# The half-swap of a rotated projection, issued on GpSimd's queue in place of the sync queue

## The chip, the cores and the metric

The kernel runs on one core of one Trainium2 chip. The metric is the device time of one execution in microseconds; the time of a kernel is the median of its runs. A core has five engines that run their own instruction streams: TensorE (PE in the profile; its weight loads are shown apart as PEld), VectorE (DVE), ScalarE (ACT), GpSimd (POOL) and SyncE (SP, which here only issues transfers). They wait for each other through semaphores. A transfer (DMA) is an instruction in the stream of the engine that issues it; the moving itself is done by 16 DMA engines, which all queues share.

## The reference

Four blocks follow each other, each with a layer norm ahead of it and added to the stream x (1024 rows of 512):

```python
x = x + attn_a(layernorm(x))      # 32 heads of 16, 8 key/value groups
x = x + ffn(layernorm(x))         # dense layer + the two best of 8 low-rank experts
x = x + attn_b(layernorm(x))      # the second attention, below
x = x + ffn(layernorm(x))
```

The change is in `attn_b`. Its weights are small whole numbers with a scale for each 128 rows of a column, its 32 query heads of 128 share 8 key/value heads, and queries and keys are rotated before the scores:

```python
w = (qw.astype(float32) - 8.0) * repeat(scales, 128, axis=0)   # _dequant_matmul
q, k, v = x @ w_q, x @ w_k, x @ w_v
def rotate_half(x):
    x1, x2 = split(x, 2, axis=-1)
    return concatenate([-x2, x1], axis=-1)
q = q * cos + rotate_half(q) * sin                             # and k the same
scores = q @ k.T / sqrt(128)                                   # causal
out = dequant_matmul(softmax(scores) @ v, qw_o, scales_o)
```

The second half of a head's 128 numbers thus has to come to where the first half stands, and the other way round.

## The kernel before

The program is one launch. The first attention and the first feed-forward block take the first 480 us or so; then the second attention begins to overlap with the end of the feed-forward block, and its heads fill the stretch from about 535 to 1350 us; the last feed-forward block follows.

**Layout.** In the second attention a projection is kept transposed: the 128 numbers of a head lie on the 128 partitions, the 1024 tokens along the free dimension, worked on in two halves of 512. Swapping the halves of the head dimension therefore means moving partitions 64 to 127 to partitions 0 to 63 and back, for 512 tokens of 4 bytes each: two transfers of 128 KB for each half of the tokens.

**One projection.** `whole_numbers` (700) loads a weight tile `r` of whole numbers on GpSimd's queue (L705) and GpSimd turns it into the number minus 8, tile `w` (L706). `r` has one buffer for each kind, `w` two. `scaled` (803) forms 512 tokens of the projection: for each of four slices of the contraction, two matmuls (the stream is held as a high and a low part; `exact`, L798 and L799) go into a PSUM bank `pp`, and the bank is multiplied by its scale into the tile `acc`, the first by ScalarE (L810), the next three by VectorE, which add (L812). `rotated` (815) does this for the two token halves: it takes an `acc` tile, forms it, swaps its halves into a tile `turned` by the two transfers L822 and L823, and then multiplies `acc` by the cosine into the result (L824), `turned` by the sine (L825) and adds (L826). These three run on GpSimd, except for query head 0, where VectorE does them. The sign of the rotation is in the sine table. `keys` (829) and `queries` (833) call `rotated`, the one for a group's key head, the other for a query head; `values` (838) uses `scaled` alone and then a ScalarE copy. There are 8 key heads and 32 query heads, two halves each: 80 pairs of transfers, 160 in all. `acc` and `turned` come from the pool `b_work`, which has two buffers of each; a buffer of `acc` is free again when the two transfers and L824 have read it, and `values` uses the same two.

**One head.** For each block t of 128 query rows, in the order 0, 6, 1, 7, 2, 4, 3, 5: scores against all keys up to the block (`probabilities` 861: matmuls L869, VectorE mask and maximum L877, ScalarE exponential L881), division (`divided` 884: L885, L886), and `placed` (890): VectorE transposes the probabilities in 32x32 blocks (L900), and for each pair of row blocks SP issues four transfers that bring the 32-row strips together (L911). `context` (936) multiplies them with the values (L949, bank `pc`) and writes the result as a high and a low part (L961, L962); `project_out` (967) multiplies with the output weights (L798 and L799 again, bank `py`) and adds to the output: VectorE L983 for three of four slices, ScalarE L987 and GpSimd L988 for the last.

**What sets the order.** TensorE's order is written out by hand: the head loop (1098) works through the row blocks and fills in between, by a cost account, from two lists: `short` (projections of coming heads and the output projections) and `long` (context products). The projection of query head n + 1 is inserted ahead of the others in head n; a key group's projection is added at the first head of a group for the next group, its values at the third. Each item is a generator; what stands in it behind a `yield` runs when it is advanced the next time, and the swap of a half stands behind the last `yield` of `scaled`. So where a query's projection is put ahead of a key's that has one half finished, this half's swap comes after the query's, and its `acc` buffer is held until then. The order on the other engines is set by the scheduler, which knows what each instruction depends on. Each engine and each queue works strictly in its own order: an instruction that waits holds up all that stand behind it.

**Queues.** On SP's queue in this stretch stand the swaps L822 and L823, the placing transfers L911 and a few others; on GpSimd's the weight loads L705, beside its own instructions L706, L824 to L826 and L988.

Of the kernel before, what the change touches and what calls it, by code (L numbers as in the profile page):

```python
# [41 lines left out]
def kernel(  # L42
# [28 lines left out]
    nc = tc.nc  # L71
# [601 lines left out]
    def attention_b():  # L673
# [5 lines left out]
        with ExitStack() as ph:  # L679
# [123 lines left out]
            def scaled(acc, w, scale, half):  # L803

                tok = ts(half, C)
                for c in range(NC_):
                    pp = ac_ps.tile([P, C], F32, tag="acc", name="pp")
                    exact(pp, w[:, c], x_hl[:, 0, c, tok], x_hl[:, 1, c, tok])
                    if c == 0:
                        nc.scalar.activation(acc, pp, AF.Copy, scale=scale(c))  # L810
                    else:
                        nc.vector.scalar_tensor_tensor(acc, pp, scale(c), acc, ALU.mult, ALU.add)  # L812
                    yield 2 * FAST

            def rotated(dst, w, scale, engines=(nc.gpsimd, nc.gpsimd)):

                for half, eng in enumerate(engines):
                    tok = ts(half, C)
                    acc = work.tile([P, C], F32, tag="acc", name="acc")
                    yield from scaled(acc, w, scale, half)  # L820
                    turned = work.tile([P, C], F32, tag="turned", name="turned")
                    nc.sync.dma_start(turned[0:64], acc[64:128])  # L822
                    nc.sync.dma_start(turned[64:128], acc[0:64])  # L823
                    eng.tensor_tensor(dst[:, tok], acc, cos_sb[:, tok], ALU.mult)  # L824
                    eng.tensor_tensor(turned, turned, sin_sb[:, tok], ALU.mult)  # L825
                    eng.tensor_tensor(dst[:, tok], dst[:, tok], turned, ALU.add)  # L826
                    yield 0

            def keys(g):
                kTs[g] = work.tile([P, S], F32, tag="kT", name=f"kT_{g}")  # L830
                yield from rotated(kTs[g], wks.pop(g), lambda c: k_sc[:, c, g : g + 1])

            def queries(n):
                qTs[n] = work.tile([P, S], F32, tag="qT", name=f"qT_{n}")
                engines = 2 * (nc.gpsimd if n else nc.vector,)
                yield from rotated(qTs[n], wqs.pop(n), lambda c: q_sc[:, c, n : n + 1], engines)
# [448 lines left out]
```

## Time and profile before

| what | value |
|---|---|
| median of 3 runs | 1445.62 us (1443.53 to 1448.45) |
| the profiled execution: time, span | 1443.47 us, 1441.6 us |
| busy over the span: PE, DVE, ACT, POOL | 1387.7, 1188.9, 868.2, 596.9 us |
| second attention, 535 to 1350 us: PE, DVE, ACT, POOL busy of 815 us | 793.62, 724.45, 541.86, 530.07 us |
| swap transfers (160), median from issue to landing | 3.1 us |
| mean granted TensorE clock | 0.994 of full speed |

Times in the profile are us from the start of the span. "L822" is line 822 of the kernel. "SPq" and "POOLq" are the queues on which SP and GpSimd issue transfers; the duration shown for a transfer in a timeline is the time for which its issue holds the issuing stream, not that of the moving. `turned<-acc` reads: writes tile `turned`, reads tile `acc`. In brackets behind an instruction stands the time that its engine was idle ahead of it, and what ended that. Weight loads of TensorE overlap its matmuls. GpSimd's busy time doesn't count its issues of transfers.

### The profile page before, as it was taken

How to read it: one execution, taken by the hardware profiler on the slowest of the kernel's cores; microseconds unless marked ns; L12 is line 12 of the kernel's file. 1: busy time of each engine (PE TensorE's matmuls, PEld its weight loads, DVE VectorE, ACT ScalarE, POOL GpSimd, SP SyncE). 2: the span in 40 equal slices, each digit the busy share in tenths (PEclk: the TensorE clock that was granted, in tenths of full speed). 3: DMA queues.
4: the chain of work that ended last, by engine and by line, in shares of the span. 5: the costliest groups of instructions: out<-in, count | busy, mean ns of one | idle time of the engine just before them, and what ended most of it. 6: DMA issues, size and time to landing. Idle time of an engine off the chain costs nothing. (4 is left out here: it accounts for less than half of the span.)

```text
span 1441.6 us, 21145 instructions
## 1 busy us (share of the span) xinstructions
PE 1387.7 (96%) x6711; PEld 882.1 (61%) x6711; DVE 1188.9 (82%) x2491; ACT 868.2 (60%) x1642; POOL 596.9 (41%) x505
## 2 busy tenths in 40 slices
PE   6999999999999998899999999999999999999888
PEld 4444444444444545677677777777777777777664
DVE  4799979979893658789898998999998998989774
ACT  2166757757677325676576676676666676666630
POOL 4200000000000616566666767657667566645230
PEclk9999999999999998999999999999999999999999
DMA  4352423324240213655566565655655655565711
GB/s 126 61 100 48 69 42 56 62 35 70 48 134 2 86 66 98 153 138 148 140 147 156 126 149 145 149 143 140 149 140 145 145 137 141 139 137 119 193 57 59
DMA packets 113183, 158.47 MB, mean 110 GB/s; under 512 B 35008, under 2 KB 86912, under 8 KB 112944
## 3 DMA queue, kind: packets, MB, share of 16 engines
q1 hardware_dynamic: 106252, 135.51, 40.3%
q0 software_dynamic: 6752, 21.57, 5.6%
q8 instruction: 54, 0.88, 0.2%
q14 instruction: 57, 0.47, 0.1%
q10 hardware_dynamic: 68, 0.03, 0.0%
HBM read 33.03 MB, written 6.05 MB: 27 GB/s over the span
## 5 line engine op out<-in xcount | busy, mean ns | idle before, releaser
L387 ACT ACTIVATE pT<-st 128x512 f32<-128x512 f32 x512 | 264.6, 603 | 128.7 <-PE st L383 109.6
L343 DVE TENSOR_REDUCE m<-sc 128x1 f32<-128x512 f32 x512 | 319.8, 682 | 25.8 <-PE st L375 19.8
L869 PE MATMUL sc<-kT,qT 128*128 128x512 f32 (+3 forms) x768 | 292.0, 489 | 2.4 <-POOL qT L826 1.3
L881 ACT ACTIVATE x_sb<-x_sb,m 128x768 f32<-128x768 f32 (+7 forms) x256 | 197.0, 769 | 120.4 <-DVE m L877 117.7
L949 PE MATMUL pc<-xT,v_sb 128*128 128x256 f32 (+1 forms) x1024 | 240.4, 361 | 14.2 <-DMA xT<-blocks 14.0
L886 ACT ACTIVATE x_sb<-x_sb,total 128x768 f32<-128x768 f32 (+7 forms) x256 | 195.5, 771 | 70.4 <-DVE total L885 69.0
L949 PEld LDWEIGHTS pc<-xT,v_sb 128*128 128x128 f32 x1024 | 190.7, 189 | 49.5 <-issue 17.2
L877 DVE CUSTOM_DVE_ANT_0 x_sb<-sc,causal 128x768 f32<-128x768 f32 (+7 forms) x256 | 191.4, 748 | 27.5 <-PE sc L869 26.1
L334 PE MATMUL sc<-ks,qs 64*128 64x512 f32 x512 | 186.7, 448 | 5.4 <-DVE m L343 2.6
L798 PE MATMUL pp<-x_hl,w 128*128 128x512 f32 x384 | 183.5, 478 | 2.2 <-ACT acc L810 1.6
L869 PEld LDWEIGHTS sc<-kT,qT 128*128 128x128 f32 x768 | 139.0, 192 | 74.5 <-issue 61.7
L383 PE MATMUL st<-ms_q,ones 64*128 64x512 f32 x512 | 178.0, 413 | 0.8 <-DMA ms_q<-mT 0.7
L375 PE MATMUL st<-qs,ks 64*128 64x512 f32 x512 | 176.0, 423 | 1.4
L334 PEld LDWEIGHTS sc<-ks,qs 64*128 64x128 f32 x512 | 83.9, 184 | 146.3 <-DVE m L343 129.6
L900 DVE STREAM_TRANSPOSE blocks<-x_sb 128x640 f32<-128x640 f32 (+3 forms) x128 | 133.2, 1041 | 27.1 <-ACT x_sb L886 21.2
L799 PE MATMUL pp<-x_hl,w 128*128 128x512 f32 x384 | 153.0, 399 | 2.2 <-DVE x_hl L756 2.2
L127 POOL DMA_DIRECT2D shared<-in_b_base_dram x1 | 0.5, 547 | 367.3 <-DVE m L343 367.3
L812 DVE SCALAR_TENSOR_TENSOR acc<-pp,q_sc,acc 128x512 f32<-128x512 f32 x192 | 140.7, 733 | 10.4 <-ACT acc L810 7.4
L706 POOL TENSOR_SCALAR w<-r 128x512 fp32r<-128x512 int32 x80 | 119.5, 1493 | 71.0 <-PE pp L799 47.0
L408 PE MATMUL po<-pT,v_sb 128*32 128x512 f32 x1024 | 136.6, 605 | 0.0
L824 POOL TENSOR_TENSOR qT<-acc,cos_sb 128x512 f32<-128x512 f32 x62 | 80.1, 1292 | 131.9 <-DVE acc L812 120.8
L798 PE MATMUL py<-ctx,w 128*128 128x512 f32 x256 | 133.0, 520 | 1.2 <-DVE xT L136 0.7
(178 smaller groups left out, 2196.8 us busy)
## 6 DMA issues: line engine op xcount, KB each, us to landing
xT<-blocks SPq DMA_DIRECT2D x128, 240.0 KB, 4.4
xT<-blocks SPq DMA_DIRECT2D x128, 176.0 KB, 3.4
turned<-acc SPq DMA_DIRECT2D x160, 128.0 KB, 3.1
pT<-x_sb SPq DMA_DIRECT2D x128, 112.0 KB, 3.6
qs<-q_hl SPq DMA_DIRECT2D x128, 64.0 KB, 2.4
qs<-shared SPq DMA_DIRECT2D x128, 64.0 KB, 2.6
r<-in_qwq_dram POOLq DMA_DIRECT2D x32, 256.0 KB, 3.6
r<-in_qwo_dram POOLq DMA_DIRECT2D x32, 256.0 KB, 3.6
```

Of the source, the lines that this page charges most:

```text
L334: nc.tensor.matmul(sc, qs[pair % NS][rows, jj, ts(t, P)], ks[pair // 2 % NS][rows, ts(half, C)], start=True, stop=True,)
L343: nc.vector.tensor_reduce(ms[pair][:, at : at + 1], sc, AX.X, ALU.max, negate=True)
L375: nc.tensor.matmul(st, ks[pair // 2 % NS][rows, ts(kt, P)], qs[pair % NS][rows, u // 2, ts(u % 2, C)], start=True, stop=False,)
L383: nc.tensor.matmul(st, ones[rows], ms_q[pair % 2][rows, u // 2, ts(u % 2, C)], start=False, stop=True)
L387: nc.scalar.activation(pTs[pair, kt][:, u], st, AF.Exp, scale=DA**-0.5)
L798: nc.tensor.matmul(ps, lhsT, high, start=True, stop=False)
L799: nc.tensor.matmul(ps, lhsT, low, start=False, stop=True)
L869: nc.tensor.matmul(sc[:, k0:k1], qT[:, ts(t, P)], kT[:, k0:k1], start=True, stop=True)
L877: nc.vector.tensor_tensor_reduce(p, sc[:, :keys], causal[:, S - keys :], -1.0, BIG, ALU.add, ALU.min, m)
L881: nc.scalar.activation(p, p, AF.Exp, bias=m, scale=-1.0, accum_out=total)
L886: nc.scalar.activation(p, p, AF.Copy, scale=total)
L949: nc.tensor.matmul(pc[:, 2 * P * i + lo : 2 * P * (i + 1)], v_sb[:, k, ts(g, DB)], some, start=(k == 0), stop=(k == 2 * pair + 1),)
```

## The change

The two transfers that swap the halves are issued by GpSimd and no longer by SP. Nothing else is edited.

```diff
@@ rotated @@
                     acc = work.tile([P, C], F32, tag="acc", name="acc")
                     yield from scaled(acc, w, scale, half)
                     turned = work.tile([P, C], F32, tag="turned", name="turned")
-                    nc.sync.dma_start(turned[0:64], acc[64:128])
-                    nc.sync.dma_start(turned[64:128], acc[0:64])
+                    nc.gpsimd.dma_start(turned[0:64], acc[64:128])
+                    nc.gpsimd.dma_start(turned[64:128], acc[0:64])
                     eng.tensor_tensor(dst[:, tok], acc, cos_sb[:, tok], ALU.mult)
                     eng.tensor_tensor(turned, turned, sin_sb[:, tok], ALU.mult)
                     eng.tensor_tensor(dst[:, tok], dst[:, tok], turned, ALU.add)
                     yield 0
```

In the scheduled program TensorE's order is the same as before. SP's order is that of before without the 160 swaps. On GpSimd each pair now stands among its other instructions, in most places right ahead of the L824 of the same half; some neighbours change places with each other by one to three, and on VectorE and ScalarE a few by up to four.

## The prediction

> **What bounds the kernel now.** I read the page first (engine shares, clock row, issues), then the table of windows over the second attention (535 to 1350 us), then the waits of that stretch, then the groups of the tile `turned`, and last the timeline at the places where TensorE stands still.
>
> ```profile
> PE 1387.7 (96%) x6711; PEld 882.1 (61%) x6711; DVE 1188.9 (82%) x2491; ACT 868.2 (60%) x1642; POOL 596.9 (41%) x505
> ...
> turned<-acc SPq DMA_DIRECT2D x160, 128.0 KB, 3.1
> ...
> r<-in_qwo_dram POOLq DMA_DIRECT2D x32, 256.0 KB, 3.6
> ```
>
> The windows, with each engine's busy us in each stretch, then granted clock, DMA share and GB/s:
>
> ```profile
> core 0: us, PE busy (x) PEld busy (x) DVE busy (x) ACT busy (x) POOL busy (x), PEclk, DMA share, GB/s
> 535.00:620.00 85.00, 74.84 (x280) 51.18 (x279) 68.56 (x144) 51.23 (x94) 52.30 (x42) 0.92 0.48 122
> ...
> 823.00:1026.00 203.00, 201.38 (x847) 150.73 (x846) 184.39 (x391) 137.23 (x256) 141.03 (x117) 1.00 0.59 145
> ...
> 1230.00:1350.00 120.00, 115.02 (x484) 85.88 (x482) 103.89 (x229) 80.42 (x151) 62.99 (x52) 1.00 0.57 134
> ```
>
> TensorE is the bound: 201.38 of 203 us in the steady state (heads run alike from about 620 to 1230 us), at full granted clock. The change moves no matmul, so it acts only through TensorE's idle time: 10 us in the first stretch, under 2 us per 203 us after it, 5 us at the end. GpSimd has 62 us free in 203.
>
> The waits of 535 to 1350 us that touch the swap or SP's queue (us in total, times, longest):
>
> ```profile
> POOL turned L825 <- DMA turned<-acc: 38.8, 26, 4.3
> ...
> PE pc L949 <- DMA xT<-blocks: 12.1, 12, 1.7
> ...
> ACT acc L810 <- DMA turned<-acc: 3.2, 5, 1.3
> ...
> PE sc L869 <- POOL qT L826: 1.3, 1, 1.3
> ```
>
> The reader sees two kinds. A late swap holds an `acc` buffer (two exist), so that L810, which starts the next projection half, waits. And the context product L949 waits for the 32x32 blocks that SP places (L911), behind the swaps on the same queue.
>
> **The change part by part.** *SP loses 160 issues, GpSimd gains them.*
>
> ```profile
> L822 SPq DMA_DIRECT2D turned<-acc x80: 461/510/662, 536.2 to 1335.7; - x80
> L823 SPq DMA_DIRECT2D turned<-acc x80: 586/596/1659, 536.7 to 1336.3; - x80
> ...
> DMA to landing us min/median/max: 2.2/3.1/4.1
> ```
>
> ```profile
> L705 POOL DMA_DIRECT2D r<-in_qwo_dram x32: 549/597/601, 489.4 to 1339.3; - x32
> ```
>
> SP is relieved of 80 x (0.510 + 0.596) = 88 us. On GpSimd no SBUF-to-SBUF transfer stands in the trace; a plain load holds its queue 0.549 to 0.601 us and a four-piece one 0.80. I take 0.55 (nearest: a plain two-dimensional transfer), bounds 0.46 (SP's shortest) and 0.80. So 1.1 us a pair and 88 us in all. Eight heads hold 20 pairs (16 query, 4 key halves): 141 + 22 = 163 of 203 us. Behind each pair L824 (1.29 us) runs, then L825 needs the landing: 0.55 + 3.1 - 1.1 - 1.29 = 1.26 us of standing still where nothing is ordered between, at most 25 us in 20 pairs: 188 of 203. GpSimd is then nearly full, but still under TensorE. What waits behind on it are L706 and L705 (weights of a coming head), L988 (the output's add) and the last of the rotation, L826. From L826 of a query's second half to the first score product of its head 4.4 to 7.8 us lie in the steady state, for a key some 45 us. I charge 1.1 to 3 us of delay against these: nothing, hidden by the running head's matmuls. Where GpSimd is already late by more than that cover, TensorE waits.
>
> *Steady state, six places.* In the third head of a group (heads 6, 10, 14, 18, 22, 26) the key's second half, finished by TensorE but not yet swapped, holds one `acc` buffer, and both query halves go through the other one. Head 14:
>
> ```profile
> 892.94 0.60 SPq L823 DMA_DIRECT2D turned<-acc  x1
> ...
> 895.76 0.69 ACT L810 ACTIVATE acc<-pp,q_sc 128x512 f32<-128x512 f32 x1
> ...
> 896.50 0.19 PEld L798 LDWEIGHTS py<-ctx,w 128*128 128x128 f32 x1 [0.81 <-ACT acc L810]
> ...
> 904.25 0.60 SPq L823 DMA_DIRECT2D turned<-acc  x1
> ...
> 911.89 1.10 PE L949 MATMUL pc<-xT,v_sb 128*128 128x256 f32 x4 [0.91 <-DMA xT<-blocks]
> ```
>
> L810 starts 2.82 us after the second swap's issue, as it lands (slack 0.0 to 0.5 us at the six). GpSimd came to this swap with 0.77 us to spare, behind the key's first half, whose own pair now puts 1.1 to 1.4 us more ahead: 0.65 late. The landing on its queue: 3.6 us (L705) against 2.7 for transfers of 256 KB on SP's says +0.9; that the swaps now pass the placing transfers on the other queue, at best from median 3.1 to 2.2, says -0.9. I take +0.6, since the placing group at 888.72 was already issued well before. Loss 1.25 us. Then SP's gain: two pairs stand on SP just before the placing at 904.95, whose transpose (L900) ended at 903.87; without them it starts up to 1.08 us sooner, and the wait at 911.89 (0.91; the six sum to 5.25) can go. I take 0.7. Net 6 x 0.55 = +3.3; bounds 6 x (0.35 - 0.9 - 0.87) = -8.5, taken as -5.25, since a wait cannot give back more than it is, and 6 x (0.65 + 0.9) = +9.3.
>
> The Trainium skill ("DMA: Bandwidth & Descriptors", Specifications) puts the first byte at some 1 us for GpSimd's path and 0.6 for SP's; an estimate by that page would be +0.4 in place of +0.6 here, 1.2 us less over the six. The trace has no GpSimd transfer of this kind to decide it.
>
> *Start, heads 0 and 1.* Here GpSimd also converts four weights, and heads wait on each other directly:
>
> ```profile
> 557.52 0.69 ACT L810 ACTIVATE acc<-pp,q_sc 128x512 f32<-128x512 f32 x1 [1.33 <-DMA turned<-acc]
> ```
>
> SP issued the key's swap at 552.85 and the query's at 555.23, each as its `acc` was ready. GpSimd in the new order ends L705 at 553.55, issues the key's pair (to 554.65), runs L824 and L706 (to 557.45) and only then the query's: 2.2 us late. So L810 at 557.52 is 0.7 late, the next one at 559.10 about 2.5, and the score product at 562.07, which already waits 0.82 us for the query's L826, 1.3. All three lie on TensorE's order: +4.5, bounds +2 (they overlap) and +7 (the granted clock here is 0.73 to 0.93 between 545 and 575 us, and longer gaps lower it further).
>
> *End, head 31.* The last query half is ready at 1332.4, but SP is in a placing group until 1335.56:
>
> ```profile
> 1335.67 0.55 SPq L822 DMA_DIRECT2D turned<-acc  x1
> ...
> 1344.10 1.77 PE L869 MATMUL sc<-kT,qT 128*128 128x512 f32 x4 [1.28 <-POOL qT L826]
> ```
>
> GpSimd is free (it runs L824 at 1332.46), so the swap is 3 us earlier and this wait goes: -1.28. Late next are the blocks (1.64 us at 1339.70), which don't depend on it.
>
> *Order.* TensorE's is the same; the scheduler moves some GpSimd, DVE and ACT instructions by one to four places (a transpose L900 four places earlier at each of the six heads). Nothing: TensorE's waits for these are 0.2 us and below apart from those above.
>
> **Sum.** +3.3 + 4.5 - 1.3 = +6.5. On the profiled execution (1443.47: span 1441.6 and 1.87 around it) that is 1449.97; it lies 2.15 under the median of three, 1445.62, so against the median 1452.1: I predict **1452**.
>
> **The rivals.** *SP's relief decides (faster).* Six waits of L949 (5.25) and head 31 (1.28) go, and the landings are as soon as SP's: 1445.6 - 6.5 = 1439. Place: L911 of the six heads. It decides if the swap at L810 lands no later than now, so that the 1.25 and the 4.5 fall away to near nothing. For it: SP holds two pairs right before the placing. Against: GpSimd works in order and came with 0.77 us to spare.
>
> *All hidden (same).* The early loss is at its least (+2), the six places come out even, the end gives 1.3: 1446.3. For it: 62 us free per 203; against: the zero slack of `acc`.
>
> *GpSimd falls behind (slower).* If issue costs 0.80 and every L825 stands 1.3 us, a pair costs 2.9: 141 + 58 = 199 of 203 us, and in the third head of a group, with three pairs, the query's second half comes later than its 4.4 us cover: some 1 us more at each of the six, plus the upper landing (9.3) and the upper start (7): 1445.6 + 6 + 9.3 + 7 - 1.3 = 1467; half of that excess gives 1460. Against: weight loads and L988 have room of a head.
>
> *Descriptors held up.* The Trainium skill ("SBUF — State Buffer", the trap that DVE blocks DMA) warns that a transfer issued by GpSimd can't have its descriptors written while some DVE instructions own a shared port. In this trace GpSimd's issues keep to 0.549 to 0.601 us beside a DVE busy 184 of 203 us, which speaks against it; no duration is taken from the page.
>
> **How the numbers follow.** No change that this kernel's measurement can tell is within 0.3%, 4.3 us: 1441.3 to 1449.9. Chances: forecast 0.45 (own range 1447 to 1457), relief 0.15, all hidden 0.20, GpSimd behind 0.20 (1457 to 1467). Faster comes from relief alone, 0.15. Same: all hidden and 0.07 of the forecast's low end, 0.27. Slower 0.58. The range leaves out the relief case's 0.15 and the last 0.05 above: 1443 to 1462.
>
> **What would show it.** Right: POOL busy near 163 in the second window; SPq without L822; waits of L810 for `turned<-acc` longer at the six heads; the 1.28 us wait at head 31 gone; the loss up to 620 us some 4 us. Wrong: the six waits of L949 gone with no new wait of L810 (relief), POOL holding an issue for 1 us or more, or L869 waiting for qT in the steady state (GpSimd behind).

## The result and the profile after

The changed kernel takes 1456.56 us (median of 4 runs, 1454.42 to 1458.36) where the kernel before takes 1444.57 on the same chip: a ratio of 1.0073, 95% interval 1.0056 to 1.0089, or 8 to 13 us slower. Differences are given by the ratio on record, here +10.5 us; the two medians alone lie 12.0 us apart. The profiled execution took 1457.05 us, with a span of 1455.2.

The page after, for engines and issues:

```profile
PE 1393.0 (96%) x6711; PEld 886.2 (61%) x6711; DVE 1192.5 (82%) x2491; ACT 869.0 (60%) x1642; POOL 682.8 (47%) x665
...
turned<-acc POOLq DMA_DIRECT2D x160, 128.0 KB, 2.6
```

GpSimd has 86 us more to do, all of it issue: contrary to what is said above, its busy time in the profile does count the transfers that it issues (160 instructions more). The median swap lands 2.6 us after its issue, against 3.1 before. The two medians don't weigh alike: the profile has a landing for all 160 swaps after, but for only 20 of them before. For the placing transfers out of `blocks` it has 30 of 256 before and 2 after, so nothing is read from their medians. The groups of the tile `turned`, with shortest, median and longest time in ns:

```profile
L822 POOL DMA_DIRECT2D turned<-acc x80: 529/552/568, 536.4 to 1343.9; - x80
L823 POOL DMA_DIRECT2D turned<-acc x80: 524/534/557, 537.0 to 1344.5; - x80
```

Where the 13.6 us between the two spans arise can be read matmul by matmul, since TensorE has the same 6711 in both, from 430 us on in the same order: subtract the start of each matmul before from its start after. The difference, worked out from the two traces:

```
matmul, its start before      starts later by
L869 (score), 562.07 us        2.96 us   (0.7 just ahead of it)
L949 (context), 589.78 us      6.37 us
L949, 592.44 us                8.02 us
L949, 604.61 us               10.15 us
L869, 608.03 us               11.52 us
L949, 620.01 us               11.54 us
L949, 1230.05 us              11.05 us
last matmul                   13.67 us
```

All of the loss but two microseconds stands in the first two heads. In the whole steady state, 610 us, the kernel gains half a microsecond. The last 2 us arise near the end, beside a granted clock of 0.83 from 1380 to 1390 us of after. They differ from execution to execution: the kernel below that leaves only the first heads on SP loses 3.5 us between 1344 us and the end in its profile, while its median is lower than that of before.

The waits of the first heads (535 to 617 us; total, times, longest), first before, then after:

```profile
PE pc L949 <- DMA xT<-blocks: 2.9, 2, 1.7
...
ACT acc L810 <- DMA turned<-acc: 2.4, 3, 1.3
...
PE sc L869 <- DVE qT L826: 0.8, 1, 0.8
```

```profile
PE pc L949 <- DMA xT<-blocks: 8.5, 2, 4.3
ACT acc L810 <- DMA turned<-acc: 8.4, 4, 4.3
...
PE sc L869 <- DVE qT L826: 3.3, 1, 3.3
```

TensorE's largest new wait is not one for a swap, but that of L949 for the placed blocks, SP's own work. The chain behind it is read in the timeline, before and after (head 0 works through its row blocks in the order 0, 1, 2, 4, 3, 5, 6, 7, so its last is the widest):

```profile
579.84 1.15 ACT L886 ACTIVATE x_sb<-x_sb,total 128x1024 f32<-128x1024 f32 x1
...
581.02 1.25 DVE L900 STREAM_TRANSPOSE blocks<-x_sb 128x1024 f32<-128x1024 f32 x1 [0.36 <-ACT x_sb L886]
...
582.26 0.69 ACT L810 ACTIVATE acc<-pp,q_sc 128x512 f32<-128x512 f32 x1 [0.89 <-DMA turned<-acc]
...
589.78 3.48 PE L949 MATMUL pc<-xT,v_sb 128*128 128x256 f32 x16 [1.23 <-DMA xT<-blocks]
```

```profile
584.49 0.69 ACT L810 ACTIVATE acc<-pp,q_sc 128x512 f32<-128x512 f32 x1 [1.45 <-DMA turned<-acc]
...
585.08 1.14 ACT L886 ACTIVATE x_sb<-x_sb,total 128x1024 f32<-128x1024 f32 x1
...
586.25 1.25 DVE L900 STREAM_TRANSPOSE blocks<-x_sb 128x1024 f32<-128x1024 f32 x1 [0.29 <-ACT x_sb L886]
...
596.15 4.09 PE L949 MATMUL pc<-xT,v_sb 128*128 128x256 f32 x11 [4.32 <-DMA xT<-blocks]
```

ScalarE's order has changed. Before, the division L886 of head 0's last row block runs first, and L810 of the next query's projection, which has to wait for an `acc` buffer, comes after it. After, L810 stands ahead: ScalarE waits for the swap's landing, and the division, the transpose L900 and the placing group wait with it. L886 is 5.2 us later, of which 3.3 are the delay that TensorE already had. The placing group, once issued, then takes 8.6 us until L949 starts, where it took 7.5 before. VectorE's order changes in the same manner: before, the transpose of head 1's first full row block (L900) precedes the write of the context's low part (L962) and a projection's L812, after, it follows them, and this L812 waits for TensorE itself:

```profile
594.92 1.25 DVE L900 STREAM_TRANSPOSE blocks<-x_sb 128x1024 f32<-128x1024 f32 x1 [1.45 <-ACT x_sb L886]
...
604.61 1.10 PE L949 MATMUL pc<-xT,v_sb 128*128 128x256 f32 x4 [1.66 <-DMA xT<-blocks]
```

```profile
601.88 0.75 DVE L812 SCALAR_TENSOR_TENSOR acc<-pp,q_sc,acc 128x512 f32<-128x512 f32 x1 [2.03 <-PE pp L799]
...
603.14 1.24 DVE L900 STREAM_TRANSPOSE blocks<-x_sb 128x1024 f32<-128x1024 f32 x1
...
614.76 2.04 PE L949 MATMUL pc<-xT,v_sb 128*128 128x256 f32 x4 [4.14 <-DMA xT<-blocks]
```

The order makes this L900 8.2 us late, little more than TensorE's delay by then. The rest of the step at 604.61 us comes behind it: from the issue of the placing group to L949 10.3 us go by, where it was 8.4.

TensorE's waits cost more than they last. After the 4.3 us gap the granted clock is half for some 3.4 us; windows after, and then the stretch behind the same wait before:

```profile
597.20:600.50 3.30, 3.30 (x10) 2.58 (x9) 1.34 (x4) 1.86 (x3) 1.37 (x2) 0.50 0.00 0
600.60:604.00 3.40, 3.40 (x17) 2.77 (x16) 2.12 (x3) 1.02 (x2) 0.00 (x0) 1.00 0.00 0
```

```profile
589.80:593.20 3.40, 3.40 (x17) 3.04 (x18) 2.56 (x4) 1.17 (x3) 2.55 (x2) 1.00 0.00 0
```

(The clock is the third number from the end; in brackets stand the instructions of each engine, TensorE first.) From 589.78 to 592.44 us (times of before) the delay grows by 1.65 us with no wait in between, and again by 1.3 us behind the second gap: together 3 of the 11.5 us.

### The profile page after: what moved, and what is told of

It reads as the page before. It is cut to its first block, busy times and chain, and to the rows that moved or that the text cites. A ratio compares the mean times of both kernels' runs of the same rounds, so it can differ in the third digit from the quotient of the medians.

```text
span 1455.2 us, 21079 instructions
## 1 busy us (share of the span) xinstructions
PE 1393.0 (96%) x6711; PEld 886.2 (61%) x6711; DVE 1192.5 (82%) x2491; ACT 869.0 (60%) x1642; POOL 682.8 (47%) x665
## 4 chain that ended last, share of the span: by engine, by line
PE 75%; DVE 10%; DMA 7%; SPq 2%; ACT 2%; POOL 2%; issue 1%; DVEq 0%; ACTq 0%; POOLq 0%
PE pc L949 15%; PE sc L869 13%; PE po L408 7%; PE sc L334 7%; DVE m L343 6%; DMA xT<-blocks 6%; PE pp L799 5%; PE pp L798 5%; PE bank L607 4%; PE py L798 3%; PE py L799 3%; SPq L911 2%; PE st L375 2%; PE py L448 2%; PE pp L268 2%; PE st L383 2%
## 5 line engine op out<-in xcount | busy, mean ns | idle before, releaser
L949 PE MATMUL pc<-xT,v_sb 128*128 128x256 f32 (+1 forms) x1024 | 244.1, 364 | 20.7 <-DMA xT<-blocks 20.2
L886 ACT ACTIVATE x_sb<-x_sb,total 128x768 f32<-128x768 f32 (+7 forms) x256 | 195.5, 771 | 78.8 <-DVE total L885 76.7
L949 PEld LDWEIGHTS pc<-xT,v_sb 128*128 128x128 f32 x1024 | 192.7, 191 | 57.2 <-issue 23.8
L900 DVE STREAM_TRANSPOSE blocks<-x_sb 128x640 f32<-128x640 f32 (+3 forms) x128 | 133.2, 1041 | 27.3 <-ACT x_sb L886 19.9
L812 DVE SCALAR_TENSOR_TENSOR acc<-pp,q_sc,acc 128x512 f32<-128x512 f32 x192 | 140.8, 734 | 11.9 <-ACT acc L810 7.3
L983 DVE SCALAR_TENSOR_TENSOR shared<-py,o_sc,shared 128x512 f32<-128x512 f32 x186 | 132.0, 728 | 4.8 <-PE py L799 4.0
```

The costliest lines, as they stand in the source:

```text
L886: nc.scalar.activation(p, p, AF.Copy, scale=total)
L949: nc.tensor.matmul(pc[:, 2 * P * i + lo : 2 * P * (i + 1)], v_sb[:, k, ts(g, DB)], some, start=(k == 0), stop=(k == 2 * pair + 1),)
```

## The experiments

All changes are in `rotated` and its two callers: a list `queues` says for each half which queue issues it, and its condition is given below. The kernel before had a median of 1446.3 to 1446.7 us beside these runs.

```diff
-                    nc.sync.dma_start(turned[0:64], acc[64:128])
-                    nc.sync.dma_start(turned[64:128], acc[0:64])
+                    queues[half].dma_start(turned[0:64], acc[64:128])
+                    queues[half].dma_start(turned[64:128], acc[0:64])
```

### Where: the first heads or the rest

```diff
 queries:  + [nc.gpsimd if n > 2 else nc.sync for h in range(2)]
 keys:     + [nc.gpsimd if g > 1 else nc.sync for h in range(2)]
```

> Swaps on GpSimd for query heads from 3 on and key heads from 2 on (68 of 80 pairs); those of the first heads stay on SP, and up to them every engine has the order of before. Theory A (the whole loss arises in heads 0 to 2, the steady state is even, head 31 gains about 1 us): 0 to -2 us against before, and no step in TensorE's starts up to 620 us. Rival B (GpSimd's extra 75 us of issue and the late landing at the six third heads cost in the steady state too): +3 us or more. Rival C (SP's relief pays): -4 us or better.

(The count in it is a slip: 10 of the 80 pairs stay on SP and 70 move.) Measured: 1443.12 against 1446.26 us, ratio 0.9986 (0.9971 to 1.0001). The 70 pairs cost nothing, and may gain some 2 us. Theory A holds; rival B, that GpSimd's extra issue costs in the steady state, falls. Rival C expected more gain than there is. This run also says how far one trace can be trusted: up to 600 us its program is that of before, and its matmuls start between 1.7 us sooner and 1.0 us later.

The counterpart moves only the other ten:

```diff
 queries:  + [nc.gpsimd if n <= 2 else nc.sync for h in range(2)]
 keys:     + [nc.gpsimd if g <= 1 else nc.sync for h in range(2)]
```

> Swaps on GpSimd for query heads 0 to 2 and key heads 0 and 1 only (10 of 12 early half-pairs' heads, 20 transfers); everything later stays on SP as before. Theory A: the whole loss, +10 to +13 us. Rival B: only a part of it, +4 to +6 us, the rest being spread over the steady state.

Measured: 1458.16 us, ratio 1.0082 (1.0064 to 1.0100), +11.9 us. One eighth of the transfers carries the whole loss.

### Which of the first ten

```diff
 early_k0q0:    queries n == 0, keys g == 0 on nc.gpsimd
 early_k1q1q2:  queries n in (1, 2), keys g == 1 on nc.gpsimd
 early_k1:      keys g == 1 on nc.gpsimd
 early_q1:      queries n == 1 on nc.gpsimd
```

> Swaps on GpSimd for key head 0 and query head 0 only (4 pairs). ScalarE has the order of before, GpSimd that of the changed kernel for these pairs. Theory A1 (the loss starts where the query's second swap stands behind two weight steps on GpSimd): the score product at 562 us is 2 to 2.5 us late, and all told +2 to +4 us. Rival A2 (what is lost at 562 us is slack that the next waits take back): 0 to +1 us.

Measured: 1448.64 us, ratio 1.0015 (0.9998 to 1.0033), +2.2 us. In its trace the score product at 562 us is 3.2 us late, and 3.3 us are still there at 590 us. A1 is right in place and size, though the interval just includes no loss. The traces of all runs agree: the product at 562 us is 1.9 to 3.2 us late in the four in which key head 0 and query head 0 move, and between 1.1 us sooner and on time in the other eight.

How the step comes about is seen in the changed kernel's trace, before and after:

```profile
559.89 0.86 DVE L825 TENSOR_TENSOR turned<-turned,sin_sb 128x512 f32<-128x512 f32 x1
...
562.07 2.50 PE L869 MATMUL sc<-kT,qT 128*128 128x512 f32 x4 [0.82 <-DVE qT L826]
```

```profile
558.71 0.57 POOL L822 DMA_DIRECT2D turned<-acc  x1
...
561.58 2.14 DVE L825 TENSOR_TENSOR turned<-turned,sin_sb 128x512 f32<-128x512 f32 x1 [0.67 <-DMA turned<-acc]
...
561.88 1.27 POOL L826 TENSOR_TENSOR kT<-kT,turned 128x512 f32<-128x512 f32 x1
...
565.03 2.29 PE L869 MATMUL sc<-kT,qT 128*128 128x512 f32 x3 [3.34 <-DVE qT L826]
```

The late swap is only the smaller part. It lets VectorE's L825 start 1.7 us later, and 0.9 of that is a delay that TensorE had before. The larger part is that L825 then takes 2.14 us where it took 0.86: GpSimd's product L826 for the key runs in the same time. (VectorE's products for query head 0 take 0.67 to 0.83 us in all 43 cases of the 13 traces in which no product of GpSimd overlaps them, and 2.13 to 2.19 us in the eight in which a whole one does.)

> Swaps on GpSimd for key head 1 and query heads 1 and 2 only (6 pairs). ScalarE's order changes as in the changed kernel: L810 of query head 1 stands ahead of the division L886 of the last row block. Theory A3 (this order and the swaps that cut into the placing transfers make the context product of head 0 wait): the waits of L949 at about 590 and 605 us grow by 2 to 3 us each, +5 to +8 us with the slower clock after them. Rival: these waits only grew because of the delay at 562 us; then 0 to +2 us.

Measured: 1454.01 us, ratio 1.0053 (1.0037 to 1.0068), +7.7 us, with no delay at 562 us. So what makes L949 wait at 590 and 605 us is a cause of its own, and the larger one.

> Swaps on GpSimd for query head 1 only (2 pairs). VectorE's order is that of before, ScalarE's but for one exchange. If the swaps cut into the placing group of head 0's last pair of row blocks (then both land together and later, where before they stood behind it on SP's queue): L949 at 590 us starts 1 to 1.5 us later, and with the following ones +1.5 to +3.5 us. If the landing is not delayed by a transfer from another queue: 0 to +0.5 us.

Measured: 1445.57 us, ratio 0.9994 (0.9981 to 1.0007). No loss; L949 at 590 us starts 0.6 us later. That a swap from another queue cuts into the placing group is not what costs here.

> Swaps on GpSimd for key head 1 only (2 pairs). ScalarE gets the changed order (L810 of query head 1 ahead of the division L886 of head 0's last row block, where it waits for an acc buffer); query head 1's swaps stay on SP, behind the placing group. If ScalarE's order is the main part: the division 1.2 to 2 us late, the placing group and L949 at 590 us as late, +2.5 to +5 us in all. If cutting in is the main part: +1.5 us at most.

Measured: 1452.89 us, ratio 1.0049 (1.0030 to 1.0067), +7.1 us, more than the +2.5 to +5 expected. Two pairs of transfers on another queue make more than half of the loss, and these are the two that change ScalarE's and VectorE's order. Query head 1's swaps are on SP here.

### The order by itself

Queue and order can be taken apart. Edges that only fix the order of issue, without a wait, put a chain of ScalarE's and VectorE's instructions of heads 0 and 1 in a given order:

```diff
+                for chain in (scalar_order, vector_order):
+                    for (a, i), (b, j) in zip(chain, chain[1:]):
+                        tc.add_manual_dep(marks[b][j].ins, marks[a][i].ins.name, mybir.DependencyInfo(mybir.DependencyClass.NoSync, mybir.DependencyReason.DATA), reason="order")
```

`marks` holds the instructions of each line as they are emitted, and the two lists, which the lines above show by a name only, hold the order as read from the scheduled kernel (before, or the one with key head 1's swaps moved).

> All swaps on SP as before; edges that only fix the order of issue put ScalarE and VectorE of heads 0 and 1 into the order that the scheduler chose where key head 1's swaps were on GpSimd. Theory D (the order of the other engines is what costs, not the queue): +5 to +8 us, and the waits of L949 at 590 and 605 us grow as there. Rival E (the queue costs: GpSimd's late issue, or the placing group in another position on SP's queue): 0 to +2 us.

Measured: 1452.04 us, ratio 1.0037 (1.0024 to 1.0051), +5.4 us, with every swap still on SP. Its timeline shows the same chain as the changed kernel's:

```profile
583.05 0.69 ACT L810 ACTIVATE acc<-pp,q_sc 128x512 f32<-128x512 f32 x1 [2.58 <-DMA turned<-acc]
...
583.63 1.14 ACT L886 ACTIVATE x_sb<-x_sb,total 128x1024 f32<-128x1024 f32 x1
...
593.97 5.22 PE L949 MATMUL pc<-xT,v_sb 128*128 128x256 f32 x12 [4.18 <-DMA xT<-blocks]
```

> Key head 1's swaps on GpSimd, with edges that keep ScalarE and VectorE in the order of before. Theory D: the +7 us of key head 1 alone fall to 0 to +1.5 us. Rival E: they stay at +5 us or more.

Measured: 1448.20 us, ratio 1.0007 (0.9995 to 1.0019). With the old order the same two pairs on GpSimd cost 1.0 us (-0.7 to +2.7) where they cost 7.1, so the edges themselves cost next to nothing. Theory D holds in both runs. The division is at its old place, and L949 too:

```profile
579.73 1.15 ACT L886 ACTIVATE x_sb<-x_sb,total 128x1024 f32<-128x1024 f32 x1
...
581.17 0.67 ACT L810 ACTIVATE acc<-pp,q_sc 128x512 f32<-128x512 f32 x1
...
589.91 3.48 PE L949 MATMUL pc<-xT,v_sb 128*128 128x256 f32 x16 [1.48 <-DMA xT<-blocks]
```

> All swaps on GpSimd as in the changed kernel, with the same edges: ScalarE and VectorE of heads 0 and 1 in the order of before. Theory D: of the loss of 11 to 12 us what remains is key head 0 and query head 0 (+2 us) less the steady state's 2 us: -1 to +3 us against before. Rival E: +8 us or more.

Measured: 1451.87 us, ratio 1.0032 (1.0018 to 1.0046), +4.6 us by the ratio where -1 to +3 was expected. Against the changed kernel's +10.5 the order gives back some 6 us; what remains is larger than theory D had it. In its trace 3.1 us stand at 562 us, as in the changed kernel, and 1.3 more at 574 us, where a score product waits 1.7 us and before had no wait. The step at 562 us is that of key head 0 and query head 0. The second is read in the timeline:

```profile
574.56 0.69 ACT L810 ACTIVATE acc<-pp,k_sc 128x512 f32<-128x512 f32 x1 [3.02 <-POOL qT L824]
...
577.27 1.07 DVE L877 CUSTOM_DVE_ANT_0 x_sb<-sc,causal 128x896 f32<-128x896 f32 x1
...
578.40 1.98 PE L869 MATMUL sc<-kT,qT 128*128 128x512 f32 x4 [1.72 <-DVE m L877]
```

GpSimd reads query head 1's second `acc` (L824) at 573.24 us, where it did so at 566.95 before: it now stands behind the swaps of that half and, between them, the rest of the first half's rotation. So L810 of key head 1 gets the buffer late. The pinned order puts this L810 ahead of a division on ScalarE; in the changed kernel the scheduler had let the division go first, and there TensorE doesn't wait at this place. The order of before is thus not the best one for every queue. This is read from one trace, and no run tests it alone.

All traces together divide by the order. From 574 to 608 us (times of before) the delay grows by 7.4 to 9.5 us in the five with the changed order (`order_only` 7.4), and by 0.3 to 1.7 us in the six that keep the order of before there; the kernel with ScalarE's queue, below, has an order of its own. The queue has a smaller share in this stretch: from the issue of the second placing group to L949 it takes 9.6 to 10.3 us in the four traces with the changed order and key head 1's swaps on GpSimd, and 8.2 to 9.1 in all others, `order_only` (8.2) among them.

### The other queue, and a selection

```diff
-                    nc.sync.dma_start(turned[0:64], acc[64:128])
-                    nc.sync.dma_start(turned[64:128], acc[0:64])
+                    nc.scalar.dma_start(turned[0:64], acc[64:128])
+                    nc.scalar.dma_start(turned[64:128], acc[0:64])
```

> All 160 swaps on ScalarE's queue: SP is relieved as in the changed kernel, GpSimd is not loaded. If what costs is GpSimd's own order at the start (weight steps ahead of a swap), this loses less than the changed kernel: 0 to +6 us. If what costs is that the swaps leave SP's queue and cut into the placing groups, or the order that the scheduler then chooses for ScalarE, it loses as much or more: +10 us and over, since ScalarE also has to issue 88 us in the middle of its exponentials.

Measured: 1473.60 us, ratio 1.0192 (1.0170 to 1.0213), +27 us. Here the loss goes on through the steady state (8 us at 680 us, 28 at 1202). There, from 630 to 1260 us, TensorE waits 13.3 us for the placed blocks and 8.5 us for ScalarE's L810. That the issues in ScalarE's stream hold up its exponentials and divisions fits this, but the order of ScalarE and VectorE changes throughout as well, so the run shows neither apart; nor does it tell the early causes apart.

```diff
 picked:  queries: nc.gpsimd if n == 31 or (n % 4 == 3 and 3 < n and h == 1) else nc.sync
          keys:    nc.gpsimd if g > 1 and h == 1 else nc.sync
```

> Swaps on GpSimd only where two pairs stood on SP right ahead of a placing group in the third head of a group (the second half of query heads 7, 11, 15, 19, 23, 27, 31 and of key heads 2 to 7) and for query head 31: 14 pairs. VectorE and ScalarE have the order of before. If SP's relief at the six places is worth what the waits there show (5.25 us) and head 31 gives 1.3: -4 to -6.5 us. If the relieved group only meets the swaps again on the DMA engines: -1.3 us (head 31 alone) to 0.

Measured: 1442.97 against 1446.48 us, ratio 0.9979 (0.9966 to 0.9992): 3.0 us faster (1.2 to 4.9), between the two expectations, and faster than both kernels. Head 31 gives nothing in its trace (2.3 us ahead of before at 1332 us, 1.8 at 1344 us); the gain arises from 620 to 1230 us. The waits from 620 to 1235 us, before and here:

```profile
PE pc L949 <- DMA xT<-blocks: 5.5, 7, 1.6
PEld py L798 <- ACT acc L810: 5.0, 6, 1.3
```

```profile
PEld py L798 <- ACT acc L810: 4.5, 6, 1.0
...
PE pc L949 <- DMA xT<-blocks: 2.7, 8, 0.6
```

About half of these waits of L949 goes. At head 14 the placing group is issued 1.0 us sooner relative to the matmuls, and 0.4 us of this is lost again between its issue and L949. That it meets the swaps, which it no longer stands behind, on the shared DMA engines would explain this, but it is not shown. (Its expectation counts 14 pairs; query head 31 brings one half more, and the halves named are 7 + 6 + 1 = 14.)

## Why the prediction was right or wrong

The forecast of 1452 us and +6.5 lies in the right direction and within the range; measured are +10.5 (8 to 13). The single terms were not right, and that the total came so near is partly luck: a loss of 3.3 us in the steady state that isn't there stands in for a loss by the changed order that was put at nothing.

- **Issue cost.** 0.55 us each was taken, 0.552 and 0.534 us were measured, and 159 to 161 us of GpSimd's time in 203 against the 163 forecast. Right.
- **Steady state, six places: +3.3.** Wrong in sign. Measured: -0.5 us over 620 to 1230 us in the one trace, and -2 us (-4 to 0) in the run that leaves only the first heads on SP. Both parts of the loss were too large. At head 14 the second swap is issued some 0.2 us late relative to the matmuls, not 0.65, and L810 starts 2.53 us after it, not 2.82 + 0.6, so that it is not late at all; the longer waits of L810 for `turned<-acc` that were to show the forecast right did not come (0.2 us from 620 to 1235 us, against 0.8). The gain by SP's relief was too large as well: the six waits of L949 fall from 5.25 to 3.6 us in sum, and some 2 us of small new waits arise elsewhere. At head 14 the placing group is issued 0.9 us sooner relative to the matmuls, and L949 waits for it longer than before:

```profile
924.02 1.10 PE L949 MATMUL pc<-xT,v_sb 128*128 128x256 f32 x4 [1.62 <-DMA xT<-blocks]
```

- **Start: +4.5, bounds +2 to +7.** Measured at 11.5 us, most of it not by this term. Of the three delays that were added up, the first two did not reach TensorE: just ahead of the score product it is 0.7 us late, no more than before the swaps. The third did: the second swap is issued at 558.71 us where 557.45 was worked out (some 1 us of this is a delay that was there before), and the score product starts 3.0 us late where 1.3 was charged, 2.3 of them new at this matmul. More than half of these 2.3 us is VectorE's longer L825, which the forecast didn't have. This is the +2 to +3 us of key head 0 and query head 0.
- **Order: nothing.** This is the step that failed. The text saw that the scheduler had moved instructions on ScalarE and VectorE, and dismissed it because TensorE's waits for these engines were short before. But the waits before are those of the order before. The change of order alone, with no transfer moved, costs 5.4 us (3.5 to 7.4).
- **End: -1.3.** The 1.28 us wait at head 31 is gone from the trace, and the delay falls by 1.4 us at that product. But the wait of L949 just ahead of it, which was taken to be independent, grows from 1.64 to 2.15 us, and the clock behind it is 0.50 where it was 1.00. So from 1335 to 1345 us nothing is gained: the delay grows by 0.6 us, and by 0.5 to 0.7 in the two other traces with head 31's swaps on GpSimd.

Of the rivals, *GpSimd falls behind* is refuted for the steady state (GpSimd's L825 waits 8.1 us for swaps from 620 to 1235 us, 23.0 before, and no score product waits for L826) and *all hidden* for the start; *SP's relief decides* is true where only the transfers that stand in front of a placing group are moved, at 3 us in place of 6.5. *Descriptors held up* doesn't show: all 160 issues keep to 524 to 568 ns beside a VectorE that is busy 184 of 203 us, and the median landing is no later, so that the trap of which the Trainium skill warns ("SBUF — State Buffer", the trap that DVE blocks DMA) shows no case in the issues here. Single swaps do land late, 20 of 160 over 4 us and the longest 6.7 us behind its issue, at 607.7 us beside a placing group; what held these was not taken apart. The Trainium skill's first-byte figures ("DMA: Bandwidth & Descriptors", Specifications) speak for a later landing on GpSimd's queue; the medians (2.6 us of 160 swaps, 3.1 us of the 20 that the profile has on SP's queue) say the opposite in this traffic, and the measurement decides.

## What to carry to other kernels

Where a scheduler sets the order, an edit on one engine can cost most on engines that it doesn't touch: compare the order of every engine before and after, and at each exchange ask whether an instruction that waits now stands ahead of one that feeds the bound. Subtracting the starts of the same matmuls in two traces says where a loss arises before any theory is needed; here it left an eighth of the transfers to look at. A queue can be relieved only where its next user waits: 14 chosen pairs gained 3 us, all 80 lost 10.5. But the 70 pairs behind the first heads gained 2 us (-4 to 0), so what the choice is shown to be worth is that it leaves out the first heads.

## What was not expected of the hardware

A transfer of 128 KB from SBUF to SBUF takes GpSimd no longer to issue (0.53 to 0.55 us in the median) than SP (0.51 to 0.60), and its median landing is no later (2.6 us, against 3.1 us for the 20 swaps on SP that the profile has); its longest is later, 6.7 against 4.1 us.

A product of VectorE can take three times as long beside one of GpSimd: 2.13 to 2.19 us in place of 0.67 to 0.83, as seen at 562 us.

A wait of TensorE that grows past some 2 us can cost another 1.6 us behind it. In the 13 traces, between 580 and 1400 us, none of the 46 waits of L949 from 1.0 to 1.86 us was followed by a lower clock in the next 5 us, 12 of the 25 from 1.86 to 2.4 us were, and all 14 longer ones. In the changed kernel such a stretch at half clock lasts 3.4 us, from 597.1 to 600.5 and from 614.2 to 617.6 us. (At L1154 and L1159, near the end, 5 of 12 waits of 1.1 us were followed by one too, so the length of the wait is not all that counts.)
